# A relational graph convolution on one core: one-hots compared four tiles at a time and weighted on another engine, with buffers, sums and limits in another order

## The chip, the cores and the metric

The kernel runs on one core of one Trainium2 chip. The metric is device time of one execution in microseconds (us). A core has a matrix engine (TensorE, PE in the profile; its weight loads are PEld), VectorE (DVE), ScalarE (ACT), GpSimd (POOL) and a queue that issues DMAs (SP). Each engine takes its own instructions in order; they wait for each other by semaphores. ACT and POOL issue DMAs from their own queues too.

## The reference

Two layers of a relational graph convolution, a residual and a layer norm. There are 12500 nodes with 128 features, 200000 edges sorted by their target, and ten relations; an edge's relation is the argmax of ten of its 42 attributes. For each node and relation the source rows are averaged, and each average is multiplied by that relation's weights:

```python
def _rgcn_layer(x, src, dst, edge_type, w_rel, root, bias):
    N = x.shape[0]
    seg = dst * NUM_REL + edge_type
    xs = x[src]
    sums = jax.ops.segment_sum(xs, seg, num_segments=N * NUM_REL)
    cnt = jax.ops.segment_sum(jnp.ones(seg.shape, x.dtype), seg, num_segments=N * NUM_REL)
    mean = (sums / jnp.maximum(cnt, 1.0)[:, None]).reshape(N, NUM_REL, -1)
    return jnp.einsum('nrd,rdo->no', mean, w_rel) + x @ root + bias
...
edge_type = jnp.argmax(msg[:, NODE_EMB_DIM:-NODE_EMB_DIM], axis=1).astype(jnp.int32)
h = jax.nn.relu(_rgcn_layer(x, src, dst, edge_type, w_rel1, root1, b1))
return _rgcn_layer(h, src, dst, edge_type, w_rel2, root2, b2)
...
x = _layernorm(x + _L0_gnn_ref(...), axis=-1)
```

## The kernel before, in words

The edges are cut into 1563 tiles of 128, one edge per partition. For each tile one indirect DMA, issued by POOL (L827, `gathered`), brings the source rows into a slot of a gather buffer `g`. A one-hot matrix `oh` has, for each edge, its weight (one over the count of its node and relation) in the column of its node and relation: the nodes of a tile span a window of 12, times ten relations gives 120 columns. PE multiplies the gathered rows with it (L1070), into one of four PSUM banks `zp` of two tiles each, and VectorE adds the product to `cc` (L860), the sums by relation, at the tile's offset. That offset is read into a register from `row` (L851), which ACT fetches once in 128 tiles.

Four tiles are a part; there are 391. The loop of `layer_1` over parts writes the order of all engines out by hand. In step p, VectorE makes the one-hots of part p + 1 (`AHEAD`), POOL gathers part p, PE multiplies part p, and VectorE adds the products of part p - 2 (`BEHIND`), half of them ahead of the step's other work and half after. That work comes from `jobs` and `todo`, lists of functions with the tile at which they are due: the preparation of the next 128 tiles' keys, weights and relations, limits for the second layer (`tile_limits`, L486, and `row_limits`), and what follows when the sums of a block of 256 nodes are complete.

A complete block is projected by PE (L820, ten relations), ACT applies the relu (L749), PE multiplies the result with the second layer's weights (L949), ACT brings these products from PSUM to a buffer (L955), and a DMA writes them to the table `TB` in DRAM. The block's place in `cc` is cleared by ACT (L800); at a lap of the ring `cc`, ACT copies its edge (L808).

From tile 177 on (`NX`), a gather takes two rows at once from `TB`: the features, and the second layer's product for that relation, if the source's block is done by then. So the same tile gives a part of the second layer's sum, with a second one-hot of 12 columns by node alone (L838 and L840, product L1074). What is left for the second layer, fewer tiles, follows in `layer_2` (one-hots L834 again, products L1529).

Gather buffers hold eight slots of 128 columns. The first 48 tiles use six buffers, the next up to tile 177 five, and from there four, with four tiles of two slots each. Every second use of a buffer takes its slots from the last to the first (`turn`). The buffers of the one-hots are four (`OB`).

`places` (L366 to L393) computes the tiles' offsets at the start; VectorE's 51 instructions of L373 are its bulk. Its result `b_r` is what `row` is fetched from.

Of the kernel before, what the change touches and what calls it, by code (L numbers as in the profile page):

```python
# [36 lines left out]
AHEAD = 1  # L37
# [33 lines left out]
def rgcn_resnorm_kernel(ctx: ExitStack, tc: tile.TileContext, x, src, dst, attr, w_rel1, root1, b1,  # L71
# [146 lines left out]
    hots_ = [lasting.tile([P, QB * KY], F32, name=f"oh{i}") for i in range(OB)]  # L218
    turn_of_ = {"g": 0, "oh": 0, "ys": 0}
# [115 lines left out]
    nodeP = in_bank(QB * WN)  # L335
# [99 lines left out]
    def shifted_rows(a, b, limit):  # L435

        first = NX // QB * QB if a == NX else a
# [37 lines left out]
    def tile_limits():  # L475
# [7 lines left out]
        for to, first in zip(reach_of, (low_of, high_of)):  # L483
            nc.vector.memset(to, 0.0)
            for i, t in enumerate(first):
                nc.vector.scalar_tensor_tensor(to, u, t - 0.5, to, op0=ALU.is_gt, op1=ALU.add)  # L486
                if i % 8 == 7:
                    yield 1
# [216 lines left out]
    zero = const.tile([P, YB], F32, name="zero")  # L705
# [124 lines left out]
    def hots(keys, weights, cols, n, m, nodes=None):  # L830
# [5 lines left out]
        if nodes is not None:  # L836
            eq = nodeP[:, :n * WN].rearrange("p (t n) -> p t n", n=WN)
            nc.vector.tensor_tensor(eq, nodes[:, :, None].to_broadcast([P, n, WN]),  # L838
                                    cols[:, None, :WN].to_broadcast([P, n, WN]), op=ALU.is_equal)
            nc.vector.tensor_tensor(oh[:, QB * KW:QB * KW + n * WN].rearrange("p (t n) -> p t n", n=WN), eq,  # L840
                                    weights[:, :, None].to_broadcast([P, n, WN]), op=ALU.mult)
# [62 lines left out]
    def layer_1():  # L904
# [107 lines left out]
        jobs.job(80 * QB, tile_limits(), 2 * QB)  # L1012
# [12 lines left out]
        for i, a in enumerate(range(0, RW, YB)):  # L1025
            def wipe(t, a=a):
                m = min(YB, RW - a)
# [3 lines left out]
        used = {}  # L1031
        turn_of_["zp"] = 0
        fixed = [ps_z.tile([P, YB], F32, name=f"zp{i}") for i in range(4)]
        for p in range(-AHEAD, NPT + BEHIND):
            if p + AHEAD < NPT:
                t0, n = parts[p + AHEAD]
                ohs[p + AHEAD] = hots(keyE[:, t0:t0 + n], wE[:, t0:t0 + n], iotaP, n, KW,
                                       nodeE[:, t0 % NODES:t0 % NODES + n] if t0 + n > NX else None)
# [3 lines left out]
            if p < NPT:  # L1042
# [16 lines left out]
                made = (g, ohs.pop(p), slot)  # L1059
            if p == NPT - CP // 4:  # L1060
                xbs[NBLK - 1] = rows_in(NBLK - 1)
                fTs[NBLK - 1] = features_in(NBLK - 1, 0, xbs[NBLK - 1])
            def products(g, oh, slot, a, b):
                n = parts[p][1]
                for j in range(a, min(b, n)):
# [6 lines left out]
                    if i >= NX:  # L1072
                        a = QB * KW + j * WN
# [658 lines left out]
```

## Time and profile before

| | us |
|---|---|
| median of 3 runs | 3123.92 |
| lowest, highest | 3121.44, 3126.94 |
| the profiled execution's own time | 3128.32 |
| its span, first to last instruction | 3126.5 |
| VectorE busy in the span | 2118.9 |
| ACT busy | 370.3 |
| POOL busy | 2296.7 |
| PE busy, and its mean granted clock | 2155.1, 0.683 of full speed |

The profile is of one execution. A row of a group gives the source line, the engine, the operation and its tiles, then the busy time and the mean of one in ns, then the time that the engine was idle just before these instructions, with what ended it (`<-`). "issue" is a wait for nothing that the profile shows. In the timeline a row gives the start, the duration, and in brackets the idle time before. Matmuls are pipelined and their ends are modelled, so a busy PE is not a PE at its peak. An fp32 product is two rows in the counts (x2 for one tile).

### The profile page before, as it was taken

How to read it: one execution, taken by the hardware profiler on the slowest of the kernel's cores; microseconds unless marked ns; L12 is line 12 of the kernel's file. 1: busy time of each engine (PE TensorE's matmuls, PEld its weight loads, DVE VectorE, ACT ScalarE, POOL GpSimd, SP SyncE). 2: the span in 40 equal slices, each digit the busy share in tenths (PEclk: the TensorE clock that was granted, in tenths of full speed). 3: DMA queues.
4: the chain of work that ended last, by engine and by line, in shares of the span. 5: the costliest groups of instructions: out<-in, count | busy, mean ns of one | idle time of the engine just before them, and what ended most of it. 6: DMA issues, size and time to landing. Idle time of an engine off the chain costs nothing.

```text
span 3126.5 us, 37701 instructions
## 1 busy us (share of the span) xinstructions
PE 2155.1 (69%) x10120; PEld 1783.0 (57%) x10120; DVE 2118.9 (68%) x8089; ACT 370.3 (12%) x602; POOL 2296.7 (73%) x2439
## 2 busy tenths in 40 slices
PE   2768787877878787888888888843655555555554
PEld 1546666666767676767676767743554444444443
DVE  6868688888777877777776868479773443434443
ACT  1112111111111111111111111100000000000000
POOL 6777777676777777777777777777777777777775
PEclk8778777776878777777777868855755555555555
DMA  6676667575666666666666655532222222222222
GB/s 183 184 216 185 200 184 232 160 215 158 200 193 196 197 194 197 196 196 196 196 185 192 184 159 146 142 94 60 60 60 63 66 70 66 67 66 70 66 67 56
DMA packets 444103, 454.59 MB, mean 145 GB/s; under 512 B 53110, under 2 KB 376239, under 8 KB 443880
## 3 DMA queue, kind: packets, MB, share of 16 engines
q0 software_dynamic: 99840, 250.04, 28.9%
q1 hardware_dynamic: 303331, 182.87, 19.6%
q10 hardware_dynamic: 40709, 19.15, 2.1%
q8 instruction: 85, 1.39, 0.2%
q14 instruction: 138, 1.13, 0.1%
HBM read 309.45 MB, written 148.80 MB: 147 GB/s over the span
## 4 chain that ended last, share of the span: by engine, by line
DVE 30%; POOL 20%; PE 19%; issue 15%; DMA 11%; DVEq 3%; ACT 1%; SPq 0%; POOLq 0%; ACTq 0%
POOL g L827 20%; DVE oh L834 8%; DVE cc L860 7%; PE pf L820 7%; DMA g<-TB,idxE 5%; PE zp L1070 4%; DVEq L851 3%; DMA g<-TB,idxB 2%; PE yb L949 2%; DMA row<-b_r 2%; PE zp L1074 2%; DVE bank L838 1%; DVE reach L486 1%; DVE acc L1554 1%; DVE cc L1274 1%
## 5 line engine op out<-in xcount | busy, mean ns | idle before, releaser
L827 POOL DMA_INDIRECT g<-TB,idxE x1563 | 1478.6, 946 | 525.8 <-issue 421.2
L1070 PE MATMUL zp<-oh,g 128*128 128x120 f32 x3126 | 822.6, 361 | 367.0 <-DVE cc L860 258.3
L1070 PEld LDWEIGHTS zp<-oh,g 128*128 128x128 f32 x3126 | 601.8, 235 | 523.9 <-DVE cc L860 354.5
L827 POOL DMA_INDIRECT g<-TB,idxB x687 | 649.1, 945 | 209.3 <-issue 199.0
L860 DVE TENSOR_TENSOR cc<-cc,zp 128x132 f32 (+1 forms) x1563 | 453.0, 290 | 373.5 <-PE zp L1074 140.7
L1529 PE MATMUL zy<-oh,g 128*128 128x12 f32 (+23 forms) x1170 | 320.3, 380 | 314.0 <-DMA g<-TB,idxB 211.5
L1074 PEld LDWEIGHTS zp<-oh,g 128*128 128x128 f32 x2772 | 529.7, 238 | 0.0
L834 DVE TENSOR_SCALAR oh<-bank,keyE,wE 128x120 f32<-128x120 f32 x1563 | 517.1, 392 | 0.0
L1529 PEld LDWEIGHTS zy<-oh,g 128*128 128x128 f32 x1170 | 274.3, 310 | 370.4 <-DMA g<-TB,idxB 230.5
L1074 PE MATMUL zp<-oh,g 128*128 128x12 f32 x2772 | 481.6, 249 | 0.0
L820 PE MATMUL pf<-cc,w 128*128 128x256 f32 (+2 forms) x1040 | 306.9, 466 | 6.3 <-DVE cc L860 5.9
L949 PE MATMUL yb<-w,a 128*128 128x512 f32 (+1 forms) x576 | 288.2, 583 | 2.3 <-ACT g L955 1.2
L820 PEld LDWEIGHTS pf<-cc,w 128*128 128x128 f32 x1040 | 250.1, 255 | 55.2 <-issue 5.8
L1529 PE MATMUL zq<-oh,g 128*128 128x16 f32 (+27 forms) x558 | 168.1, 395 | 155.6 <-DMA g<-TB,idxB 141.4
L1529 PEld LDWEIGHTS zq<-oh,g 128*128 128x128 f32 x558 | 138.2, 314 | 188.6 <-DMA g<-TB,idxB 154.2
L827 POOL DMA_INDIRECT g<-in_x_dram,idxE x177 | 167.4, 946 | 74.3 <-issue 50.6
L777 DVE TENSOR_TENSOR cc<-pf,cc 128x256 f32<-128x256 f32 (+2 forms) x52 | 21.2, 409 | 264.4 <-PE pf L1472 264.3
L1554 DVE TENSOR_TENSOR acc<-acc,zy 128x12 f32 (+25 forms) x585 | 104.3, 178 | 105.3 <-PE zy L1529 50.7
L834 DVE TENSOR_SCALAR oh<-columns,keyB,wB 128x15 f32<-128x15 f32 (+25 forms) x687 | 163.8, 322 | 0.1
L783 ACT ACTIVATE rstd<-mv,eps 128x2 f32<-128x2 f32 (+2 forms) x52 | 15.3, 295 | 967.1 <-DVE mv L781 967.0
L749 ACT ACTIVATE a<-pf,b 128x256 f32<-128x256 f32 (+1 forms) x50 | 23.3, 466 | 852.9 <-PE pf L822 852.9
L800 ACT ACTIVATE cc<-zero 128x1280 f32<-128x1280 f32 x90 | 118.8, 1368 | 4.8 <-DVE acc L942 4.8
(265 smaller groups left out, 1807.3 us busy)
## 6 DMA issues: line engine op xcount, KB each, us to landing
TB<-xb SPq DMA_DIRECT2D x88, 640.0 KB
m<-in_edge_attr_dram SPq DMA_DIRECT2D x48, 672.0 KB
TB<-g SPq DMA_DIRECT2D x98, 256.0 KB
g<-TB,idxE POOLq DMA_INDIRECT x1563
TB<-ys SPq DMA_DIRECT2D x96, 256.0 KB
g<-TB,idxB POOLq DMA_INDIRECT x687
TB<-ys SPq DMA_DIRECT2D x49, 128.0 KB
TB<-in_x_dram ACTq DMA_DIRECT2D x12, 512.0 KB
```

The source lines that it names most:

```text
L486: nc.vector.scalar_tensor_tensor(to, u, t - 0.5, to, op0=ALU.is_gt, op1=ALU.add)
L800: nc.scalar.activation(cc[:, r, o:o + n], zero[:, None, :n].to_broadcast([P, m, n]), AF.Copy)
L820: nc.tensor.matmul(po[:, :n], wsb[l][:, r, :], sums[:, r], start=(r == 0), stop=(w is None and r == NREL - 1))
L827: nc.gpsimd.indirect_dma_start(out=g[:, j * C:(j + n) * C], out_offset=None, in_=table, in_offset=bass.IndirectOffsetOnAxis(ap=idx, axis=0))
L834: nc.vector.tensor_scalar(oh[:, j * m:(j + 1) * m], cols[:, :m], keys[:, j:j + 1], weights[:, j:j + 1], op0=ALU.is_equal, op1=ALU.mult)
L851: vals = nc.values_load_multi_w_load_instructions(row, engines=[DVE], min_val=min(a for a, _ in lims), max_val=max(b for _, b in lims), sk ...
L860: nc.vector.tensor_tensor(s, s, zp[:, at:at + m * w].rearrange("c (r n) -> c r n", n=w), op=ALU.add)
L949: nc.tensor.matmul(yb[:h, :m], fin_a[k][:, b * P:b * P + h], wsb[1][:, r:r + m // C, :], start=True, stop=True)
L1070: nc.tensor.matmul(zp[:, o:o + KW], g[:, slot[j] * C:(slot[j] + 1) * C], oh[:, j * KW:(j + 1) * KW], start=True, stop=True)
L1074: nc.tensor.matmul(zp[:, o + KW:o + KY], g[:, (slot[j] + 1) * C:(slot[j] + 2) * C], oh[:, a:a + WN], start=True, stop=True)
L1529: nc.tensor.matmul(zp[:, j * w:(j + 1) * w], g[:, at * C:(at + 1) * C], oh[:, j * w:(j + 1) * w], start=True, stop=True)
L1554: nc.vector.tensor_tensor(s, s, zps[q][:, j * w:(j + 1) * w], op=ALU.add)
```

## The change

Layer 1's one-hots are made in two steps by two engines. `ones` (L842 in the changed kernel) compares the keys of four tiles with the column numbers in one VectorE instruction of 480 columns. `weighted` (L850) then multiplies each tile's 120 columns in place with the edge's weight, on ACT, from the last tile to the first. The comparison runs two parts ahead (`AHEAD` = 2), the weighting one. The one-hots by node get buffers of their own, two, and are made for eight tiles at once (L858 and L860), once in two parts.

All four sums of part p - 2 now stand ahead of the step's other work: two, then the comparison, then two. `finished` keeps what follows them at its old place in PE's order. Gathers of single rows take their slots forwards always. Tile limits are done in groups of four every fourth part, where they were groups of eight every second. The fills with zeros at the start take 256 columns each, where they took 512. Layer 2 has no change of its own.

```diff
-AHEAD = 1
+AHEAD = 2
...
-    hots_ = [lasting.tile([P, QB * KY], F32, name=f"oh{i}") for i in range(OB)]
+    hots_ = [lasting.tile([P, YB], F32, name=f"oh{i}") for i in range(OB)]
+    nhots_ = [lasting.tile([P, 2 * QB * WN], F32, name=f"nh{i}") for i in range(2)]
...
-                if i % 8 == 7:
+                if i % 4 == 3:
                     yield 1
...
-    zero = const.tile([P, YB], F32, name="zero")
+    zero = const.tile([P, BN], F32, name="zero")
...
-    def hots(keys, weights, cols, n, m, nodes=None):
+    def hots(keys, weights, cols, n, m):
...
+    def ones(keys, n):
+
+        oh = next_of("oh", hots_)
+        nc.vector.tensor_tensor(oh[:, :n * KW].rearrange("p (t m) -> p t m", m=KW),
+                                iotaP[:, None, :].to_broadcast([P, n, KW]),
+                                keys[:, :, None].to_broadcast([P, n, KW]), op=ALU.is_equal)
+        return oh
+
+    def weighted(oh, j, w):
+
+        s = oh[:, j * KW:(j + 1) * KW]
+        nc.scalar.activation(s, s, AF.Copy, scale=w)
+
+    def node_hots(t0):
+
+        n = min(2 * QB, NT - t0)
+        a = t0 % NODES
+        oh = next_of("nh", nhots_)
+        eq, to = [b[:, :n * WN].rearrange("p (t n) -> p t n", n=WN) for b in (nodeP, oh)]
+        nc.vector.tensor_tensor(eq, nodeE[:, a:a + n, None].to_broadcast([P, n, WN]),
+                                iotaP[:, None, :WN].to_broadcast([P, n, WN]), op=ALU.is_equal)
+        nc.vector.tensor_tensor(to, eq, wE[:, t0:t0 + n, None].to_broadcast([P, n, WN]), op=ALU.mult)
         return oh
...
-        jobs.job(80 * QB, tile_limits(), 2 * QB)
+        jobs.job(80 * QB, tile_limits(), 4 * QB)
...
         for p in range(-AHEAD, NPT + BEHIND):
+            t = p * QB
+            if 0 <= p < NPT - 1:
+                sums(p, t, 0, 2)
             if p + AHEAD < NPT:
                 t0, n = parts[p + AHEAD]
-                ohs[p + AHEAD] = hots(keyE[:, t0:t0 + n], wE[:, t0:t0 + n], iotaP, n, KW,
-                                       nodeE[:, t0 % NODES:t0 % NODES + n] if t0 + n > NX else None)
+                ohs[p + AHEAD] = ones(keyE[:, t0:t0 + n], n)
+            if 0 <= p + AHEAD - 1 < NPT:
+                t0, n = parts[p + AHEAD - 1]
+                for j in reversed(range(n)):
+                    weighted(ohs[p + AHEAD - 1], j, wE[:, t0 + j:t0 + j + 1])
+            if 0 <= p < NPT - 1:
+                sums(p, t, 2, QB)
+            if p % 2 and p + 1 < NPT and parts[p + 1][0] + QB > NX // (2 * QB) * 2 * QB:
+                nhs[(p + 1) // 2] = node_hots(parts[p + 1][0])
...
-                if not plain or p % 2 == 0:
+                if not plain:
                     turn = used[id(g)] = 1 - used.get(id(g), 1)
-                slot = [p % 2 * QB + j if plain else 2 * j for j in range(n)]
-                if turn:
-                    slot = [GQ - (1 if plain else 2) - a for a in slot]
+                slot = [p % 2 * QB + j if plain else 2 * (n - 1 - j if turn else j) for j in range(n)]
...
             if p < NPT - 1:
-                sums(0, 2)
                 products(*made, 0, 2)
                 todo.run(t - QB // 2)
                 jobs.run(t)
-                sums(2, QB)
+                finished(p, t)
                 products(*made, 2, QB)
```

**VectorE, one step in the middle of layer 1, before.** The step in which a chunk's counts become weights (`wp`); `zp_406` holds the third and fourth tile of part p - 2, `oh_90` is the one-hot buffer of part p + 1, L444 ends the relations of 16 tiles ahead, L636 to L639 are jobs.

```order
L444 ISA idxE<-idxE,moved 128x32
L636 TENSOR_REDUCE cn<-pf 128x128
L638 TENSOR_SCALAR cn<-cn 128x128
L639 RECIPROCAL wp<-cn 128x128
L860 ISA
L860 TENSOR_TENSOR cc<-cc,zp_406 128x11x12
L860 ISA
L860 TENSOR_TENSOR cc<-cc,zp_406 128x11x12
L834 TENSOR_SCALAR oh_90<-bank,keyE,wE 128x120 x4
L838 TENSOR_TENSOR bank<-nodeE,bank 128x48
L840 TENSOR_TENSOR oh_90<-bank,wE 128x48
```

**VectorE, the same step in the changed kernel**, from the load of the offsets (L870) to the first of the same jobs (L431); `zp_430` and `zp_431` are the two banks of part p - 2, and `oh_90` is the buffer of part p + 2.

```order
L870 TENSOR_LOAD row
L879 ISA
L879 TENSOR_TENSOR cc<-cc,zp_430 128x11x12
L879 ISA
L879 TENSOR_TENSOR cc<-cc,zp_430 128x11x12
L842 TENSOR_TENSOR oh_90<-bank,keyE 128x480
L879 ISA
L879 TENSOR_TENSOR cc<-cc,zp_431 128x11x12
L879 ISA
L879 TENSOR_TENSOR cc<-cc,zp_431 128x11x12
L431 TENSOR_SCALAR movedf<-keyE 128x16
```

The second pair of sums stood behind the step's jobs and now stands ahead of them; one comparison of 480 columns stands between the pairs in place of four instructions of 120 after them, and the pair of 48 columns is gone from this step.

**ACT around a finished block of 256 nodes, before** (`fT` the block's features, `a` the relu behind its projection, `ys` and `g` the buffers of the second layer's products).

```order
L800 ACTIVATE cc<-zero 128x6x256
L990 ACTIVATE fT<-pf 128x256
L749 ACTIVATE a<-pf,b_385 128x256
L955 ACTIVATE ys_106<-yb 128x512
L955 ACTIVATE ys_107<-yb 128x512
L955 ACTIVATE g_89<-yb 128x256
```

**ACT around such a block in the changed kernel** (`oh_90` to `oh_93` the one-hot buffers of four parts in turn).

```order
L801 ACTIVATE cc<-zero 128x6x256
L850 ACTIVATE oh_93<-oh_93,wE 128x120 x4
L1009 ACTIVATE fT<-pf 128x256
L850 ACTIVATE oh_90<-oh_90,wE 128x120 x4
L850 ACTIVATE oh_91<-oh_91,wE 128x120 x4
L850 ACTIVATE oh_92<-oh_92,wE 128x120 x4
L750 ACTIVATE a<-pf,b_410 128x256
L850 ACTIVATE oh_93<-oh_93,wE 128x120 x4
L974 ACTIVATE ys_108<-yb 128x512
L974 ACTIVATE ys_109<-yb 128x512
L850 ACTIVATE oh_90<-oh_90,wE 128x120 x4
```

Four weightings for each part now stand between the instructions that follow PE, in the same queue.

**VectorE at the start, before**: the first chunk's weights, then `places` (L366 and on), into which the first one-hots are laid one by one; the pattern of the last rows goes on for 16 one-hots.

```order
L636 TENSOR_REDUCE cn<-pf 127x128
L638 TENSOR_SCALAR cn<-cn 127x128
L639 RECIPROCAL wp<-cn 127x128
L286 COPY wE<-pf 128x127
L366 TENSOR_TENSOR off<-b_i,even 13x128
L369 MEMSET lows 13x128
L834 TENSOR_SCALAR oh_90<-bank,keyE,wE 128x120
L373 SCALAR_TENSOR_TENSOR lows<-even,lows 13x128
```

**VectorE at the start in the changed kernel.**

```order
L618 TENSOR_TENSOR eqb<-bank,kh 127x1344 x5
L842 TENSOR_TENSOR oh_90<-bank,keyE 128x480
L842 TENSOR_TENSOR oh_91<-bank,keyE 128x480
L637 TENSOR_REDUCE cn<-pf 127x128
L842 TENSOR_TENSOR oh_92<-bank,keyE 128x480
L639 TENSOR_SCALAR cn<-cn 127x128
L842 TENSOR_TENSOR oh_93<-bank,keyE 128x480
L640 RECIPROCAL wp<-cn 127x128
L287 COPY wE<-pf 128x127
L367 TENSOR_TENSOR off<-b_i,even 13x128
L370 MEMSET lows 13x128
L374 SCALAR_TENSOR_TENSOR lows<-even,lows 13x128 x46
```

The comparisons need no weights, so they moved ahead of them, and nothing stands between the instructions of `places` any more.

More of the change, by code (lines that the diff above doesn't have):

```diff
@@ L1072, in products @@
                     if i >= NX:
[L1073 to L1074 removed]
+                        a = (i % (2 * QB)) * WN
+                        nc.tensor.matmul(zp[:, o + KW:o + KY], g[:, (slot[j] + 1) * C:(slot[j] + 2) * C], nh[:, a:a + WN],
                                          start=True, stop=True)
[L1077 to L1102 removed]
             if p < NPT - 1:
[L1105 removed]
                 products(*made, 0, 2)
@@ L1112, in layer_1 @@
                 jobs.run(t)
-                sums(0, QB)
+                sums(p, t, 0, QB)
+                finished(p, t)
                 if p < NPT:
```

79 lines of the change are left out of this document (38 added, 41 removed).

## The prediction, made before the changed kernel had run

> **What bounds the kernel now.** I read the page's span and groups first, then a table by stage, then POOL's own timeline and waits, and last the stretch around POOL's longest wait. The gathers are the groups to begin with; the columns are line, engine, operation, tiles and count, then busy time and mean ns, then the idle time ahead of them.
>
> ```profile
> span 3126.5 us, 37701 instructions
> PE 2155.1 (69%) x10120; PEld 1783.0 (57%) x10120; DVE 2118.9 (68%) x8089; ACT 370.3 (12%) x602; POOL 2296.7 (73%) x2439
> L827 POOL DMA_INDIRECT g<-TB,idxE x1563 | 1478.6, 946 | 525.8 <-issue 421.2
> L827 POOL DMA_INDIRECT g<-TB,idxB x687 | 649.1, 945 | 209.3 <-issue 199.0
> L827 POOL DMA_INDIRECT g<-in_x_dram,idxE x177 | 167.4, 946 | 74.3 <-issue 50.6
> ```
>
> A gather holds POOL 0.945 us. Where nothing stops it (the second layer, x687) 209.3/687 = 0.305 us lie ahead of each, called issue: one gather per 1.250 us. All 1563 + 687 + 177 = 2427 then need 3034 us of a span of 3126.5. POOL, busy 73% by the page, is within 3% of being the only bound, and a gain is at most what POOL loses beyond that pace. The table says where it does (stretch and length, then busy us and counts, PE's granted clock, DMA share, GB/s):
>
> ```profile
> 390.00:790.00 400.00, 315.40 (x1597) 262.26 (x1596) 334.99 (x1324) 63.56 (x94) 275.41 (x292) 0.75 0.65 190
> 790.00:1700.00 910.00, 748.52 (x3880) 631.92 (x3880) 694.84 (x2505) 159.07 (x233) 686.84 (x727) 0.77 0.66 195
> 1700.00:1910.00 210.00, 175.69 (x873) 145.85 (x874) 161.84 (x566) 34.62 (x52) 152.20 (x161) 0.76 0.57 164
> 2060.00:3100.00 1040.00, 537.43 (x1916) 440.56 (x1917) 543.30 (x2361) 17.52 (x54) 786.51 (x833) 0.52 0.25 64
> ```
>
> POOL's count is the fifth bracket. Lost time is length minus count times 1.250: 400 - 365 = 35 us in the first row, 910 - 909 = 1 in the second, 210 - 201 = 9 in the third, nothing in the fourth (833 gathers fit to the edge). So the second layer has nothing to give or lose, and layer 1 lost 45 us in two stretches. The rest is at two points:
>
> ```profile
> 83.14 0.94 POOL L827 DMA_INDIRECT g<-in_x_dram,idxE  x1 [19.06 <-PE zp L1070]
> 2040.77 0.94 POOL L827 DMA_INDIRECT g<-TB,idxE  x1 [3.19 <-DMA rowP<-b_i]
> 3105.82 0.94 POOL L827 DMA_INDIRECT g<-TB,idxB  x1 [0.30 <-issue]
> ```
>
> The start costs 19.06 - 0.30 = 18.8 us, the change of layers 2.9. After the last gather come 3126.5 - 3105.8 = 20.7 us of tail. Lost in all: 18.8 + 35 + 1 + 9 + 3 = 67 us. Who holds POOL in the first stretch:
>
> ```profile
> POOL g L827 <- PE zp L1074: 36.2, 16, 7.6
> 540.45 0.78 PE L1070 MATMUL zp<-oh,g 128*128 128x120 f32 x2 [5.15 <-DVE cc L860]
> 551.87 6.54 PE L820 MATMUL pf<-cc,w 128*128 128x256 f32 x20
> 559.91 0.94 POOL L827 DMA_INDIRECT g<-TB,idxE  x1 [7.55 <-PE zp L1074]
> ```
>
> 16 waits of 36.2 us are for a product to free a gather buffer (four buffers of four tiles: a lead of 16 tiles, 20 us). PE was late because VectorE's sums (L860) were late with the PSUM banks, 5.15 us at one wait, and a block's projection (6.54 us) then came on top. VectorE is busy 335 of 400 us there and 695 of 910 (76%) in the next stretch, where POOL loses 1 us. Its load is what tells the two apart: the clock (0.75, 0.77) does not.
>
> **The one-hots.** Per part (four tiles) VectorE loses four compares and, once relations are split by node, two small products. The rows:
>
> ```profile
> 1006.75 1.32 DVE L834 TENSOR_SCALAR oh<-bank,keyE,wE 128x120 f32<-128x120 f32 x4
> L838 DVE TENSOR_TENSOR bank<-nodeE,bank 128x48 f32<-128x48 f32 x347 | 73.7, 212 | 11.8
> L840 DVE TENSOR_TENSOR oh<-bank,wE 128x48 f32<-128x48 f32 x347 | 71.9, 207 | 11.9
> L617 DVE TENSOR_TENSOR eqb<-bank,kh 128x1344 bf16<-128x1344 f32 (+2 forms) x65 | 100.7, 1551 | 1.3 <-PE pf L628 0.7
> L486 DVE SCALAR_TENSOR_TENSOR reach<-u,reach 128x6 f32<-128x6 f32 x252 | 42.2, 167 | 7.6
> ```
>
> The new compare is the form of L838 and L617 (both operands broadcast or stepped, one from PSUM) with 480 columns; no row has that width. Between 48 and 1344 columns a column costs (1551 - 212)/1296 = 1.03 ns, so 212 + 432 x 1.03 = 0.66 us; bounds are 0.21 and 1.55. I take 0.66, by the line through both. It saves 1.32 - 0.66 = 0.66 us a part; at 1.55 it would lose 0.23. Node one-hots for eight tiles at once cost 2 x (0.21 + 48 x 0.00103) = 0.52 us instead of 4 x 0.21, which saves 0.16 a part. Together 0.82 us of the 5.0 us that four gathers take. The tile limits (L486, 42.2 us) were done in steps of 8 every second part and now come in steps of 4 every fourth: of those 42 us about 30 leave the stretch for later parts.
>
> So VectorE has in 390 to 790: 335 - 73 parts x 0.82 - 30 = 245 of 400 us, 61%, below the 76% at which POOL loses 1 us in 910. In 1700 to 1910: 162 - 40 x 0.82 = 129 of 210, 61% as well (77% before). Sums of a part's third and fourth tile also move ahead of the step's other jobs, so PE's second half no longer waits behind those. I leave 4 of the 35 us and 2.5 of the 9 standing, for blocks where PE itself is late: 31 + 6.5 saved.
>
> **ACT's new work**, 1563 activations of 128x120 with a scale per partition. Nearest rows:
>
> ```profile
> L749 ACT ACTIVATE a<-pf,b 128x256 f32<-128x256 f32 (+1 forms) x50 | 23.3, 466 | 852.9 <-PE pf L822 852.9
> L990 ACT ACTIVATE fT<-pf 128x256 f32<-128x256 f32 (+1 forms) x50 | 18.6, 373 | 150.5 <-PE pf L983 150.5
> 2036.88 0.30 ACT L1202 ACTIVATE cc<-zero 127x128 f32<-127x128 f32 x1
> 2037.08 0.30 ACT L1203 ACTIVATE cc<-zero 127x128 f32<-127x128 f32 x1
> 393.32 0.60 ACT L955 ACTIVATE g<-yb 128x512 f32<-128x512 f32 x1 [5.25 <-PE yb L949]
> ```
>
> Two zero fills follow each other here: 2037.08 - 2036.88 = 0.20 us is the pitch of such short operations, the lower bound; 0.47 us (L749, twice as wide, a column operand as here) is the upper. L749 over L990 puts the column operand at 0.09 us, so I take 0.30: 1.2 us a part (0.8 to 1.9), of 5.0. ACT's 370 us on the page become some 840, 40% of layer 1. It is covered because the compare runs two parts ahead and the weighting one: a product finds weights that ACT began a part earlier. Queued behind a waiting ACT instruction (the relu behind a projection, an eviction that waits up to 5.25 us for PE) are the weights of a part whose products stand one to three parts further on in PE's order; without that cover 1.2 us would fall on PE in every part.
>
> **The start.** The 49th gather goes to the second buffer. Before, the slots were taken backwards there, so it waits for the product of tile 15; now forwards, for tile 8.
>
> ```profile
> 53.38 0.38 DVE L834 TENSOR_SCALAR oh<-bank,keyE,wE 128x120 f32<-128x120 f32 x1
> 53.89 0.38 DVE L834 TENSOR_SCALAR oh<-bank,keyE,wE 128x120 f32<-128x120 f32 x1
> 54.21 9.67 DVE L373 SCALAR_TENSOR_TENSOR lows<-even,lows 13x128 f32<-13x128 f32 x31
> 73.67 0.59 DVE L860 TENSOR_TENSOR cc<-cc,zp 128x120 f32 x2 [5.11 <-issue]
> 74.31 1.21 PE L1070 MATMUL zp<-oh,g 128*128 128x120 f32 x4 [23.30 <-DVE cc L860]
> 81.65 1.21 PE L1070 MATMUL zp<-oh,g 128*128 128x120 f32 x4 [1.52 <-DVE cc L860]
> ```
>
> Tiles 8 and 9 are the products at 74.31, tiles 14 and 15 those at 81.65. The first sum waits for the places of the tiles (L373 and on). 16 one-hots stood between these, each adding 0.51 - 9.67/31 = 0.20 us: 3.2 us. The four compares now stand ahead: two in a wait for PE, two (1.3 us) before the weights are done. So the first sum comes at 73.67 - 1.9 = 71.8, and tile 8's product ends 0.64 + 0.61 later, at 73.0: gather 49 starts some 9.5 us earlier (bounds: 0, if ACT's weights come late, and 18.8). Later tiles follow at less than the 1.25 us a gather needs, so it stays. Short wipes of zeros (256 columns instead of 512) lie on ACT before 46 us, when nothing waits for ACT: no cost, or up to 1.2 us, one part's weights.
>
> **Sum:** 9.5 + 31 + 6.5 = 47 us off the span. The profiled execution took 3128.3 us (span 3126.5), the median of the runs is 3123.9; taken off that: 3077 us.
>
> **Rivals.** *PE keeps the bound (3104).* Two speeds stand in the rows:
>
> ```profile
> 716.39 0.78 PE L1070 MATMUL zp<-oh,g 128*128 128x120 f32 x2 [3.89 <-DVE cc L860]
> 733.50 0.46 PE L1070 MATMUL zp<-oh,g 128*128 128x120 f32 x2
> L1074 PE MATMUL zp<-oh,g 128*128 128x12 f32 x2772 | 481.6, 249 | 0.0
> L820 PE MATMUL pf<-cc,w 128*128 128x256 f32 (+2 forms) x1040 | 306.9, 466 | 6.3 <-DVE cc L860 5.9
> L949 PE MATMUL yb<-w,a 128*128 128x512 f32 (+1 forms) x576 | 288.2, 583 | 2.3 <-ACT g L955 1.2
> ```
>
> Slow, four tiles take 4 x 0.78 = 3.1 us; L1074, L820 and L949 add (482 + 307 + 288)/391 parts = 2.8 us a part, so a PE that stayed slow would need 5.9 of the 5.0 us that there are. If PE, waiting less for VectorE, waits for gathers instead and stays slow, only a quarter of the 37.5 us goes: 3124 - 9.5 - 10 = 3104. Against it: from 790 to 1700 the clock is the same and POOL loses 1 us. [...]
>
> *ACT's queue becomes the bound (slower, 3169).* If the weights come more than a part (5.0 us) behind the compare, because they sit behind evictions that wait for PE, PE waits at the next part and POOL loses its lead. One part's weights and an eviction, 1.2 + 0.6 us, at each of 50 blocks (x50 at L749) are 92 us: 3077 + 92 = 3169. For it: ACT already waits up to 5.25 us at an eviction, and its instructions run in one order. Against it: ACT is busy 64 of 400 us now, and the queue order leaves two parts.
>
> *It does not do what it says (3124).* The compare at 1.1 us or more leaves VectorE's load where it was, and the start's wait only moves.
>
> **How the numbers follow.** Forecast 0.66, by itself 3064 (both stretches wholly won, 44 us, and 16 at the start) to 3092 (two thirds of the 47); PE's bound 0.17; no effect 0.05; ACT's queue 0.12. Range 3060 to 3116: it holds nearly all of the first two (0.63 + 0.17), and so leaves out 0.20. What this kernel's runs can tell from no change is about 0.2%, 6 us. Faster 0.83, same 0.05, slower 0.12.
>
> **What would show it.** Right: a compare of about 0.66 us (L842) and four weightings within 1.2 us; gather 49 near 73.5 us; 390 to 790 with some 316 gathers; POOL's waits for the products (L1132, which is L1074 before) below 10 us there; the last 1040 us unchanged. Wrong: POOL or PE waiting for L850, a VectorE busy over 75% in 390 to 790, or the same waits for products with the clock at 0.75 or less.

## The result, and the profile after

| | before | after |
|---|---|---|
| median, us | 3123.75 (4 runs) | 3076.23 (4 runs) |
| lowest, highest | 3121.44, 3126.94 | 3074.45, 3076.94 |
| span of the profiled execution | 3126.5 | 3075.1 |

The ratio is 0.9846, with a 95% interval of 0.9829 to 0.9863: 47.5 us faster, where 47 were forecast. The page of the changed kernel begins as follows (busy time, share of the span, instructions), and its groups for gathers, compare, weights and products have the columns of the rows shown before:

```profile
span 3075.1 us, 38388 instructions
PE 2162.1 (70%) x10120; PEld 1810.3 (59%) x10120; DVE 1782.8 (58%) x6571; ACT 824.8 (27%) x2190; POOL 2296.1 (75%) x2439
...
L828 POOL DMA_INDIRECT g<-TB,idxE x1563 | 1478.5, 946 | 487.5 <-issue 407.6
L1128 PE MATMUL zp<-oh,g 128*128 128x120 f32 x3126 | 825.2, 362 | 317.0 <-DMA g<-TB,idxE 183.9
...
L850 ACT ACTIVATE oh<-oh,wE 128x120 f32<-128x120 f32 x1563 | 482.1, 383 | 217.4 <-DVE oh L842 198.5
...
L842 DVE TENSOR_TENSOR oh<-bank,keyE 128x480 f32<-128x480 f32 x391 | 255.3, 653 | 399.4 <-PE zp L1128 365.4
```

VectorE has lost 336 us of work and ACT has gained 454. A compare of 480 columns takes 653 ns (0.66 us was the estimate). The gather is what it was, 946 ns, and POOL's busy time too (2296.1 us, 2296.7 before): all that was won was POOL's waiting. The table by stretches, with the columns of the one before (POOL's count is the fifth bracket):

```profile
390.00:790.00 400.00, 330.57 (x1699) 283.02 (x1698) 247.54 (x877) 158.66 (x413) 298.79 (x316) 0.76 0.69 202
790.00:1700.00 910.00, 765.88 (x3920) 655.42 (x3920) 576.81 (x1992) 367.50 (x958) 686.76 (x727) 0.75 0.66 194
1700.00:1910.00 210.00, 184.59 (x920) 154.41 (x920) 118.59 (x389) 85.90 (x228) 158.86 (x168) 0.76 0.58 165
2010.00:3050.00 1040.00, 534.66 (x1904) 437.96 (x1904) 540.85 (x2360) 17.53 (x54) 786.28 (x833) 0.52 0.25 64
```

Between 390 and 790 there are now 316 gathers, so 400 - 316 x 1.25 = 5 us are lost there; 727 fit in the second row as before, 168 x 1.25 fill the third, and layer 2 has the same 833. POOL's longest waits that are left, and the last gather, stand in the timeline (start, duration, the idle time ahead in brackets):

```profile
70.50 0.94 POOL L828 DMA_INDIRECT g<-in_x_dram,idxE  x1 [6.49 <-PE zp L1128]
...
535.08 0.94 POOL L828 DMA_INDIRECT g<-TB,idxE  x1 [5.03 <-PE zp L1132]
...
1989.10 0.94 POOL L828 DMA_INDIRECT g<-TB,idxE  x1 [4.19 <-DMA rowP<-b_i]
...
3054.42 0.94 POOL L828 DMA_INDIRECT g<-TB,idxB  x1 [0.30 <-issue]
```

| POOL's loss, us | before | forecast after | after |
|---|---|---|---|
| start (49th gather) | 18.8 | 9.3 | 6.2 |
| 390 to 790 | 35 | 4 | 5 |
| 790 to 1700 | 1 | 1 | 1 |
| 1700 to 1910 | 9 | 2.5 | 0 |
| change of layers | 2.9 | 2.9 | 3.9 |
| after the last gather | 20.7 | 20.7 | 20.7 |

The rows add up to a gain of 51 us; the spans differ by 51.4. (A window that is the same in us holds somewhat later tiles in the changed kernel, which is over 40 us ahead by 1700.) PE's waits before layer 1's products show why the stretches closed (what is waited for, us in all, times, the longest). First the kernel before, then the changed one:

```profile
PE zp L1070 <- DVE cc L860: 258.3, 205, 23.3
...
PE zp L1070 <- DMA g<-TB,idxE: 93.0, 92, 2.8
```

```profile
PE zp L1128 <- DMA g<-TB,idxE: 183.9, 191, 3.6
...
PE zp L1128 <- DVE cc L879: 30.0, 29, 2.4
PE zp L1128 <- ACT oh L850: 12.4, 11, 1.6
```

PE waited 258 us for VectorE's sums; now it waits 30 us for them, 12 us for ACT's weights, and mostly, 184 us, for the gathers, which at 1.25 us each take 3034 of the span's 3075.1 us. A part of the fall is a change of name: PE's first long wait at the start, 23.3 us and put down to the sums before, is still there with 18.3 us, but is called issue. In all, PE's idle time ahead of these products fell from 367.0 to 317.0 us.

### The profile page after: what moved, and what is told of

Its sections match the earlier page's. It is cut to its first block, busy times and chain, and to the rows that moved or that the text cites. A ratio compares the mean times of both kernels' runs of the same rounds, so it can differ in the third digit from the quotient of the medians.

```text
span 3075.1 us, 38388 instructions
## 1 busy us (share of the span) xinstructions
PE 2162.1 (70%) x10120; PEld 1810.3 (59%) x10120; DVE 1782.8 (58%) x6571; ACT 824.8 (27%) x2190; POOL 2296.1 (75%) x2439
## 4 chain that ended last, share of the span: by engine, by line
PE 31%; POOL 22%; DMA 16%; issue 15%; DVE 13%; ACT 2%; DVEq 1%; POOLq 0%; ACTq 0%; SPq 0%
POOL g L828 22%; DMA g<-TB,idxE 11%; PE zp L1128 10%; PE pf L821 9%; PE yb L968 4%; PE zp L1132 4%; DMA g<-TB,idxB 3%; DVE cc L879 2%; DMA row<-b_r 1%; DVE oh L835 1%; DVEq L870 1%; DVE acc L1585 1%; DVE cc L1305 1%; PE pf L1340 1%; PE pf L627 1%
## 5 line engine op out<-in xcount | busy, mean ns | idle before, releaser
L1128 PE MATMUL zp<-oh,g 128*128 128x120 f32 x3126 | 825.2, 362 | 317.0 <-DMA g<-TB,idxE 183.9
L1128 PEld LDWEIGHTS zp<-oh,g 128*128 128x128 f32 x3126 | 614.1, 239 | 453.1 <-issue 149.9
L1132 PEld LDWEIGHTS zp<-nh,g 128*128 128x128 f32 x2772 | 543.8, 244 | 0.0
L850 ACT ACTIVATE oh<-oh,wE 128x120 f32<-128x120 f32 x1563 | 482.1, 383 | 217.4 <-DVE oh L842 198.5
L1132 PE MATMUL zp<-nh,g 128*128 128x12 f32 x2772 | 491.0, 252 | 0.0
L842 DVE TENSOR_TENSOR oh<-bank,keyE 128x480 f32<-128x480 f32 x391 | 255.3, 653 | 399.4 <-PE zp L1128 365.4
L750 ACT ACTIVATE a<-pf,b 128x256 f32<-128x256 f32 (+1 forms) x50 | 23.3, 465 | 439.2 <-PE pf L823 439.2
```

Source lines behind the costliest of these rows:

```text
L842: nc.vector.tensor_tensor(oh[:, :n * KW].rearrange("p (t m) -> p t m", m=KW), iotaP[:, None, :].to_broadcast([P, n, KW]), keys[:, :, None] ...
L850: nc.scalar.activation(s, s, AF.Copy, scale=w)
L1128: nc.tensor.matmul(zp[:, o:o + KW], g[:, slot[j] * C:(slot[j] + 1) * C], oh[:, j * KW:(j + 1) * KW], start=True, stop=True)
L1132: nc.tensor.matmul(zp[:, o + KW:o + KY], g[:, (slot[j] + 1) * C:(slot[j] + 2) * C], nh[:, a:a + WN], start=True, stop=True)
```

## The experiments

Twelve runs followed, of ten kernels, on four chips; the table keeps the runs of one chip together. On none of these did the kernel before take the time of the first measurement: its medians there are 3777, 3817, 3827 and 3778 us. The last two sections come back to that. So whole times are compared within one chip only, and the mechanism is read from places that are the same on all chips (the start) or from waits.

The waits have a limit of their own. The profile names what ended a wait from the records of semaphores, and the twelve traces hold 16584 to 18679 of these, where the first two hold 59558 and 60986. That a wait whose record is missing may be called issue or remote, or go by another name, is my guess and was not tested; to be safe, a sum of waits by name in the twelve is not to be set against one of the first two traces. Between traces of the same steady code such sums scatter too: on one chip PE waits 62.4 us for the weights in changed_again and 86.9 in places_early, and on two chips 182.9 and 136.2 us for ACT's evictions (the moves of the second layer's products out of PSUM) in the changed kernel itself.

| kernel | median, us | before, same chip | ratio, 95% interval |
|---|---|---|---|
| undo_turn | 3762.4 | 3777.3 | 0.9963 (0.9947 to 0.9979) |
| undo_limits | 3755.9 | 3777.3 | 0.9938 (0.9917 to 0.9960) |
| undo_sums | 3754.9 | 3777.3 | 0.9929 (0.9904 to 0.9955) |
| hots_alone | 3768.7 | 3777.3 | 0.9987 (0.9970 to 1.0003) |
| changed_again | 3808.0 | 3817.3 | 0.9986 (0.9970 to 1.0002) |
| three_compares | 3856.5 | 3817.3 | 1.0102 (1.0077 to 1.0126) |
| act_twice | 3855.8 | 3817.3 | 1.0110 (1.0090 to 1.0130) |
| places_early | 3810.6 | 3817.3 | 0.9986 (0.9970 to 1.0002) |
| hots_alone_2 | 3834.3 | 3827.4 | 1.0026 (1.0006 to 1.0046) |
| orders_alone | 3819.4 | 3827.4 | 0.9983 (0.9963 to 1.0002) |
| weights_early | 3756.9 | 3778.4 | 0.9932 (0.9906 to 0.9957) |
| changed_third | 3749.9 | 3778.4 | 0.9920 (0.9896 to 0.9943) |

**One part of the change undone.** undo_turn takes the slots as before, undo_limits the old pace of the limits, undo_sums the old place of a part's second two sums; hots_alone undoes all three, and keeps the new one-hots. Each by its core:

```diff
-                slot = [p % 2 * QB + j if plain else 2 * (n - 1 - j if turn else j) for j in range(n)]
+                slot = [p % 2 * QB + j if plain else 2 * j for j in range(n)]
+                if turn:
+                    slot = [GQ - (1 if plain else 2) - a for a in slot]
```

```diff
-                if i % 4 == 3:
+                if i % 8 == 7:
...
-        jobs.job(80 * QB, tile_limits(), 4 * QB)
+        jobs.job(80 * QB, tile_limits(), 2 * QB)
```

```diff
-            if 0 <= p < NPT - 1:
-                sums(p, t, 2, QB)
...
                 jobs.run(t)
+                sums(p, t, 2, QB)
                 finished(p, t)
```

> The changed kernel with the slots of the single-row gathers taken backwards at every second use again. Theory (the 49th gather waits for the product of tile 15 instead of tile 8): the wait before gather 49 grows from 6.5 us to 11 to 14 us, nothing else changes, about 6 us slower (ratio to before 0.986 to 0.988). Rival (the start was won by the comparisons that left the chain of the places, the slots give nothing): the wait stays at 6.5 us, ratio 0.984 to 0.985.

> The changed kernel with the tile limits in groups of eight every second part again, so that all 42 us of them fall between 400 and 770 us. Theory (VectorE's share of the stretch decides, and the one-hots alone lower it enough): VectorE about 275 of 400 us in 390 to 790 (69%), POOL loses 5 to 10 us there instead of 5, ratio 0.984 to 0.987. Rival (the spreading of the limits is what freed the stretch): POOL loses 15 us or more there, ratio 0.988 or above.

> The changed kernel with the second pair of sums behind the step's jobs again. Theory (the load decides, not the order): POOL loses at most 5 us more in 390 to 790, ratio 0.984 to 0.986. Rival (PE's second half was late because its bank came behind the jobs): POOL loses 15 us or more more, ratio 0.989 or above.

> The changed kernel with all three undone (slots, limits, order of the sums): of the change only the one-hots in two steps, the node one-hots for eight tiles and the shorter fills are left. Theory (the one-hots' relief of VectorE carries the stretches): POOL's loss in 390 to 790 is 5 to 12 us, the start loses 11 to 16 us, ratio 0.987 to 0.990. Rival (the orders carry it): POOL loses 25 us or more in 390 to 790, ratio 0.994 or above.

The whole times expected were for a chip at 3124 us, and cannot be held against these. All four are faster than before or level with it. Among the first three, undo_limits and undo_sums are level; hots_alone is slower than both (its interval lies above theirs). What each undone part costs cannot be told, since the changed kernel itself did not run on that chip. What the traces show is the start and PE's waits; both are read below, with the counterpart.

**The one-hots alone again, and the orders alone.** orders_alone is the kernel before with the changed slots, limits and place of the sums, and its own one-hots:

```diff
-                if i % 8 == 7:
+                if i % 4 == 3:
...
-        jobs.job(80 * QB, tile_limits(), 2 * QB)
+        jobs.job(80 * QB, tile_limits(), 4 * QB)
...
-                slot = [p % 2 * QB + j if plain else 2 * j for j in range(n)]
-                if turn:
-                    slot = [GQ - (1 if plain else 2) - a for a in slot]
+                slot = [p % 2 * QB + j if plain else 2 * (n - 1 - j if turn else j) for j in range(n)]
...
                 sums(0, 2)
+                sums(2, QB)
                 products(*made, 0, 2)
```

> The new one-hots and ACT's weights with the old slots, the old pace of the limits and the old order of the sums, for the second time. Where the kernel before takes about 3124 us: VectorE has 247.5 + 30 = 278 of 400 us between 390 and 790 (69%, still below the 76% at which POOL lost 1 us in 910), so by the theory (VectorE's load sets that stretch) POOL loses at most 10 us there, and at the start some 6 us more than in the changed kernel, as gather 49 waits for tile 15 again: 3080 to 3090 us. Rival (the order and the slots made the gain): over 3105 us. Where the kernel before takes over 3700 us: within 10 us of it, as the first time (ratio 0.999).

> The counterpart: the kernel before with its own one-hots on VectorE, but with the changed slots, the limits spread over twice the parts, and the sums of a part's third and fourth tile ahead of the step's other jobs. Where the kernel before takes about 3124 us: the start gains 6 us by the slots; VectorE has 335 - 30 = 305 of 400 us between 390 and 790 (76%), at the edge of what POOL bore from 790 on, so by the theory 10 to 25 of the 35 us lost there go: 3093 to 3108 us, above the kernel with the one-hots alone. Rival (the one-hots made nearly all of it): 3112 to 3120 us. Where the kernel before takes over 3700 us, the undone limits and sums alone seemed worth -10 to -15 us there, so 0 to 15 us above the kernel before.

On this chip the orders alone come out 8 us below the kernel before, where 0 to 15 above were expected, and the one-hots alone 7 us above it. The orders alone are thus the faster by 15 us, with intervals that do not meet: that the one-hots are the part with the gain is not what times on this chip show.

The start, from the timelines: the issue of the row that the first sum needs, the first sum, the 49th gather. The changed kernel of the first measurement (its 49th gather, at 70.50, is shown above); then changed_again, undo_turn, undo_sums, hots_alone_2 and orders_alone:

```profile
65.39 0.58 ACTq L1058 DMA_DIRECT2D row<-b_r  x1
...
68.78 0.59 DVE L879 TENSOR_TENSOR cc<-cc,zp 128x120 f32 x2 [3.42 <-issue]
```

```profile
87.37 0.58 ACTq L1058 DMA_DIRECT2D row<-b_r  x1
...
92.47 0.95 POOL L828 DMA_INDIRECT g<-in_x_dram,idxE  x1 [28.59 <-PE zp L1128]
```

```profile
88.10 0.58 ACTq L1058 DMA_DIRECT2D row<-b_r  x1
...
98.62 0.94 POOL L828 DMA_INDIRECT g<-in_x_dram,idxE  x1 [34.76 <-PE zp L1130]
```

```profile
87.67 0.58 ACTq L1058 DMA_DIRECT2D row<-b_r  x1
...
92.77 0.95 POOL L828 DMA_INDIRECT g<-in_x_dram,idxE  x1 [28.93 <-PE zp L1126]
```

```profile
87.55 0.58 ACTq L1058 DMA_DIRECT2D row<-b_r  x1
90.94 0.59 DVE L879 TENSOR_TENSOR cc<-cc,zp 128x120 f32 x2 [3.42 <-issue]
...
100.62 0.95 POOL L828 DMA_INDIRECT g<-in_x_dram,idxE  x1 [36.63 <-PE zp L1128]
```

```profile
90.63 0.60 ACTq L1083 DMA_DIRECT2D row<-b_r  x1
...
95.55 1.29 DVE L860 TENSOR_TENSOR cc<-cc,zp 128x120 f32 x4 [4.96 <-issue]
...
97.25 0.94 POOL L827 DMA_INDIRECT g<-in_x_dram,idxE  x1 [33.43 <-PE zp L1068]
```

From the row to the 49th gather it is 5.11 us in the changed kernel of the first measurement and 5.10 in changed_again: the traces differ before the row, not after it. So the start can be taken apart. Before it was 83.14 - 68.59 = 14.55 (row issue in that trace at 68.59). The one-hots alone leave 13.07 (1.5 won: the first sum follows the row by 3.4 us instead of 5). The sums' place then brings 13.07 to 10.52 (2.5), the slots 10.52 to 5.10 (5.4, where 4.5 to 7.5 were expected). These two are not independent: undo_sums, which has the changed slots and the old place of the sums, has 5.10 as well. With the slots forwards the 49th gather does not need the second pair of sums, and the slots alone win all 8 us there; two gathers later the old place costs 0.9. The row itself comes 90.63 - 87.55 = 3.1 us earlier with the new one-hots, on one chip. Together 12.5 us, and 83.14 - 70.50 = 12.6 were won in the first measurement. orders_alone gives the slots and the sums' place together from the other side: 97.25 - 90.63 = 6.62 is 14.55 less 7.9, and 2.5 + 5.4 = 7.9.

PE's waits for the sums, of orders_alone, hots_alone_2, undo_sums, undo_turn and three_compares (the changed kernel with each compare made three times; it comes next) in this order:

```profile
PE zp L1068 <- DVE cc L860: 229.5, 70, 23.1
```

```profile
PE zp L1128 <- DVE cc L879: 71.2, 38, 7.7
```

```profile
PE zp L1126 <- DVE cc L879: 85.1, 53, 4.2
```

```profile
PE zp L1130 <- DVE cc L879: 12.1, 7, 4.0
```

```profile
PE zp L1134 <- DVE cc L885: 28.0, 24, 3.7
```

Without the new one-hots the changed orders leave 230 us of waits for sums. With them 71 are left (87.5 in the first run of hots_alone), and with the sums' new place as well about 10 (12.1 in undo_turn; undo_limits has 9.2 and the changed kernel itself 3.4 and 11.1 in its two runs). So the new one-hots and the sums' place both take these waits away, and the slots and the pace of the limits do not touch them.

That it is VectorE's load which makes them, as the theory has it, these traces speak against. three_compares keeps VectorE busy for 2289.6 us, orders_alone for 2122.4, and yet the first has 28.0 us of such waits and the second 229.5 (on two chips, whose times for the kernel before differ by 10 us). What else tells the two apart is the order: with the old one-hots VectorE makes a part's one-hots (1.32 us, and twice 0.21 for those by node) right ahead of its four sums; with the new ones two sums come first, and the compare is made two parts ahead. No run takes order and load apart any further, and none has VectorE as full as it was in the first measurement: 335 of the 400 us from 390 on there, 282 of the same 400 in three_compares. Nor do these waits set the time on these chips: undo_sums, with 85 us of them, and undo_limits, with 9, take 3754.9 and 3755.9 us on the same chip. PE's idle time moves there rather than goes. Ahead of layer 1's products and ahead of the second layer's it is, on one chip, in orders_alone and then in hots_alone_2:

```profile
L1068 PE MATMUL zp<-oh,g 128*128 128x120 f32 x3126 | 851.7, 371 | 375.9 <-DVE cc L860 229.5
L949 PE MATMUL yb<-w,a 128*128 128x512 f32 (+1 forms) x576 | 372.6, 736 | 204.5 <-ACT g L955 90.0
```

```profile
L1128 PE MATMUL zp<-oh,g 128*128 128x120 f32 x3126 | 859.9, 375 | 275.4 <-issue 112.3
L968 PE MATMUL yb<-w,a 128*128 128x512 f32 (+1 forms) x576 | 367.9, 728 | 340.5 <-ACT g L974 141.4
```

The one-hots alone have 100 us less than the orders alone at the first, and 136 us more at the second.

**VectorE's load, ACT's load, and the places earlier.** three_compares makes each compare three times, act_twice follows each weighting by a second activation, places_early calls `places` ahead of the counts of the first 128 tiles:

```diff
                                 keys[:, :, None].to_broadcast([P, n, KW]), op=ALU.is_equal)
+        nc.vector.tensor_tensor(oh[:, :n * KW].rearrange("p (t m) -> p t m", m=KW),
+                                iotaP[:, None, :].to_broadcast([P, n, KW]),
+                                keys[:, :, None].to_broadcast([P, n, KW]), op=ALU.is_equal)
+        nc.vector.tensor_tensor(oh[:, :n * KW].rearrange("p (t m) -> p t m", m=KW),
+                                iotaP[:, None, :].to_broadcast([P, n, KW]),
+                                keys[:, :, None].to_broadcast([P, n, KW]), op=ALU.is_equal)
```

```diff
         nc.scalar.activation(s, s, AF.Copy, scale=w)
+        nc.scalar.activation(s, s, AF.Copy, scale=1.0)
```

```diff
     checked(0, d_f)
+    places()
     pc = None
...
-    places()
     weights_in()
```

> The changed kernel itself, beside the others of this call, so that they are read against it on one and the same chip. Where the kernel before takes about 3124 us, 3076 us again (ratio 0.985). Where it takes about 3777 us, as in the first four experiments, POOL waits of some 4 us per 24 gathers run through both layers; if these leave the change its own part of the gain, 3777 - 48 = 3729 us; if they cover part of it (the four undone versions gained 9 to 22 us there), 3740 to 3756 us.

> Slots, limits, order of sums and ACT's weights as in the changed kernel, but each part's compare is made three times: 2 x 0.653 = 1.31 us more of VectorE per part, 79 parts in the 400 us from 390 on, so VectorE's 247.5 us there become some 350 of 400 (88%; the kernel before had 335), and in the 910 us after it 577 + 182 x 1.31 = 815 (90%; before 695). Theory (VectorE's load set the loss between 390 and 790): POOL loses at least the 35 us of before there and now loses in the next stretch too, so at least 3076 + 30 + 10 = 3116 us, up to 3160. Rival (the slots, the limits' pace and the order of the sums made the gain, VectorE's load is covered): within 6 us of the changed kernel.

> Each weighting on ACT is followed by a second activation of the same tile: ACT's 0.29 to 0.38 us per tile become twice that, 2.5 us a part instead of 1.25, ACT's busy time 825 us becomes some 1300 (about 65% of layer 1). Theory (ACT has slack, the weights are made a part ahead): within 6 us of the changed kernel, with the start up to 2.5 us later. Rival (ACT's queue is close to the bound): PE waits for the weights at each block, 50 blocks x 1 to 2 us: 50 to 100 us slower.

> The places of the tiles (46 small VectorE operations, 14.4 us) are worked out before the counts of the first chunk rather than after them, so that they, and the row that the first sum loads, no longer come last before the first sum. Theory (the 6.2 us that POOL still waits ahead of the 49th gather are a chain of VectorE work, row, first sum, product): the weights come up to 14 us later, the sums' places are no longer the last; if the weights of the first parts then come before the row did, gather 49 starts up to 6 us earlier, 3070 us (6 under the changed kernel). Rival (the weights now end last: the same VectorE work stands ahead of the first product either way): no change within 6 us, with PE's first product later and its wait at gather 49 as long as before.

The second rows of the pages of changed_again, three_compares and act_twice:

```profile
PE 2184.9 (57%) x10120; PEld 1840.8 (48%) x10120; DVE 1787.3 (47%) x6571; ACT 823.3 (22%) x2190; POOL 2302.3 (60%) x2439
```

```profile
PE 2199.5 (57%) x10120; PEld 1844.8 (48%) x10120; DVE 2289.6 (59%) x7353; ACT 827.8 (21%) x2190; POOL 2296.3 (59%) x2439
```

```profile
PE 2153.5 (56%) x10120; PEld 1815.2 (47%) x10120; DVE 1786.1 (46%) x6571; ACT 1286.4 (33%) x3753; POOL 2295.8 (60%) x2439
```

502 us more of VectorE cost 48 us at the end, which lies in the theory's range of 40 to 84 over the changed kernel; the rival, VectorE's load being covered, falls. But the cost did not come the way the theory has it. PE's waits for the sums are 28.0 us instead of 3.4; its waits for ACT's evictions are 234 instead of 183, while ACT waits 254 us for the compares instead of 90. That the late compares held ACT's queue, and the evictions in it, would explain this, and was not tested. 463 us more of ACT cost 48 us too: there the theory was wrong and the rival nearly right. PE's waits for the weights in changed_again, then in act_twice:

```profile
PE zp L1128 <- ACT oh L850: 62.4, 21, 6.2
```

```profile
PE zp L1129 <- ACT oh L851: 133.3, 41, 6.9
```

In act_twice another 26.9 us are waits for the first of the two activations (L850). On these chips ACT's queue does hold PE (62.4 us in changed_again), at an engine that is busy 22% of the span there. An estimate from these runs follows. A us of VectorE's work is worth 48/502 = 0.096 us there, and one of ACT's 48/463 = 0.104. The change takes 336 us from VectorE and gives ACT 454, so these two come to -32 + 47 = +15 us, against 12.6 won at the start: little in all. Measured are -9 us on one chip and -28 on another, and hots_alone at -9 and +7. The estimate explains that the gain is smaller than 47.5 us, and no more.

places_early moved nothing: its row is issued at 87.45 us (87.37 in changed_again), and gather 49 starts at 92.55 (92.47). 27 of the 46 operations still ran behind the counts in VectorE's order, so it tells neither for nor against a start bound by the places.

**The weights a part earlier.**

```diff
-            if 0 <= p + AHEAD - 1 < NPT:
-                t0, n = parts[p + AHEAD - 1]
+            if p + AHEAD < NPT:
                 for j in reversed(range(n)):
-                    weighted(ohs[p + AHEAD - 1], j, wE[:, t0 + j:t0 + j + 1])
+                    weighted(ohs[p + AHEAD], j, wE[:, t0 + j:t0 + j + 1])
```

> ACT weights a part in the step in which VectorE compares it, two parts ahead of its products instead of one. On the chips of the experiments PE waits 62 us for the weights (21 times, up to 6.2 us), and 133 us where each weighting is followed by a second activation, which made the kernel 48 us slower: there 0.67 us of the end per us of PE's wait. Theory (part of what the new one-hots save is given back because the weights stand behind evictions in ACT's queue): with 5 us more lead PE's wait for weights falls below 25 us, and the kernel is 15 to 30 us faster than the changed kernel of the same call. Rival (ACT's stalls, not its order, take the time; and ACT, now waiting for the compare of the same step, delays the evictions behind it): no gain, PE's waits for the evictions (183 us) grow by what those for the weights lose, within 8 us of the changed kernel. Where the kernel before takes about 3124 us PE waits only 12.4 us for the weights: within 5 us of 3076 us.

> The changed kernel, for the comparison with the weights a part earlier. 3076 us where the kernel before takes 3124; where it takes over 3750 us, 0.994 to 1.000 of that.

PE's waits for ACT in changed_third, then in weights_early:

```profile
PE yb L968 <- ACT g L974: 81.8, 21, 6.6
PE yb L968 <- ACT ys L974: 54.4, 18, 7.2
PE zp L1128 <- ACT oh L850: 49.1, 21, 6.2
```

```profile
PE yb L968 <- ACT ys L974: 94.4, 25, 7.6
PE yb L968 <- ACT g L974: 86.4, 23, 7.0
...
PE zp L1127 <- ACT oh L850: 13.5, 7, 5.5
PE zp L1127 <- DVE cc L879: 56.2, 21, 8.7
```

The waits for the weights fall by 36 us, as the theory said, and the gain it forecast does not come: the median is 7 us above the changed kernel's, with intervals that overlap. The rival's forecast holds. Its reason is less sure. The waits for the evictions are 45 us longer than in changed_third, but at 181 us no longer than in changed_again (183); and the waits for the sums grew as much, from 11.1 to 56.2 us. So what the weights won was lost at other waits, and one trace of each does not tell at which. No kernel that ran beside the changed one on its chip beats it.

## Why the prediction was right

**The bound.** Right. POOL's busy time (2296.7 and 2296.1 us) and the pace of a gather (833 in 1040 us of layer 2 both times) did not move, and the gain is the sum of its waits (51 us of 51.4 in the span).

**The one-hots, 31 us.** Right in size: 35 to 5 us in that stretch, VectorE at 247.5 us there (245 forecast). PE's waits for sums went as the prediction has it in the first two traces (258.3 to 30.0 us). Its reason, VectorE's load, is not shown: three_compares has more load than orders_alone (2289.6 us against 2122.4) and an eighth of its waits for sums (28.0 against 229.5), which points to what stands ahead of the sums in VectorE's order. The 30 us of limits that I moved out of the stretch are not seen to matter: undoing their pace left PE's waits at 9 us. The place of the sums did (85 to about 10), and the prediction named it without a size of its own. That PE's waits for the sums made the 30 us of POOL's loss was not tested by an experiment on a chip at 3124 us; it rests on the two first traces.

**The late stretch, 6.5 us.** It won all 9: VectorE fell to 118.6 of 210 us, not 129. What made this loss no run shows by itself.

**The start, 9.5 us.** The mechanism was right, the term too small: 12.6. The row came 3.2 us earlier (68.59 to 65.39), where 1.9 was taken, since the four compares did not lengthen VectorE's way to the row (the weights were copied at 45.65, and at 45.79 before); and the first sum followed the row by 3.4 us instead of 5.1, which was not foreseen. In both traces of kernels with the old one-hots ACT's queue issued two transfers of 512 KB right behind the row (row at 68.59 us, transfers at 69.27 and 69.87 before; 90.63, 91.30 and 91.90 in orders_alone); with the new ones four weightings (1.25 us) and a fill (0.40) stand between. That these slowed the row's transfer is a guess; no run tests it.

**ACT.** Four weightings in 1.25 us (1.2 forecast), 824.8 us on the page (840). Its queue held PE for 12.4 us in all, so the rival of 3169 us did not come. (By its own terms it was 3167: 50 blocks at 1.8 us are 90 us, not 92.) On the four other chips PE's waits for the weights were 46 us and more wherever the weights stood as in the changed kernel, so it came there in part.

**The sum.** 47 us were to come off the span, 51.4 did. That the median still came out within a us is luck: the profiled execution of before took 4.4 us more than its median, and that of the changed kernel 0.7 more. Within the sum the start was 3 us too small and the late stretch 2.5, while the long stretch and the change of layers came out a us worse each. What was confirmed is the way of counting POOL's losses by place.

**The rivals.** PE's slow speed: from 390 to 790 the clock was 0.76 (0.75 before) and POOL was not held (5 us lost); over all of layer 1 PE waited twice as long for gathers as before (183.9 us against 93.0), and its products took 362 ns (361 before). What remains of POOL's waits for products between 390 and 790 is 11.4 us in 21 waits, a little over the 10 that were named as a sign, and 6 of it is the usual 0.30 us ahead of a gather. The longest, 5.0 us at 535.08, follows a block's projection (6.92 us from 526.66), which came after ACT had copied the ring's edge (1.78 us from 520.85). That the change does nothing: excluded by the interval.

## What to carry to other kernels

Where one engine's fixed pace is within a few per cent of the whole time, list its waits by stretch and ask for each which engine is late there. The load of that engine in a stretch that loses nothing gave a forecast of the right size here, but not a cause: ask also what stands ahead of the late instruction in its engine's order. Work that is moved to an idle engine is not free because its share is low: it goes into a queue with others (ACT was busy 12% of the span before; the weights that it was given then held PE for 12.4 us, and for 62.4 in changed_again). And a gain holds for the conditions under which the bound was read: 47.5 us became 9 and 28 in two later measurements, so measure before and after more than once, on more than one chip.

## What the runs showed of the hardware that was not expected

The same program took 3076 us in the first measurement, 3808 on one chip and 3750 on another. Most instructions are as long (the compare 653 and 654 ns, the gather 946 and 949 in the first measurement and in changed_again); PE's products of layer 1 took 362 and 370 ns, at a mean granted clock of 0.679 and 0.654. Layer 2's gathers, in code that no edit touched, have 344.8 us of idle time ahead of them in changed_again, where the first measurement had 209:

```profile
L828 POOL DMA_INDIRECT g<-TB,idxB x687 | 650.3, 947 | 344.8 <-issue 196.6 <-remote 80.6 <-PE zy L1560 38.7
```

VectorE there waits for what the profile cannot name ("remote"), in groups that waited for nothing of the kind in the first trace:

```profile
DVE oh L842 <- remote: 264.2, 79, 10.6
DVE acc L1585 <- remote: 250.3, 63, 14.4
DVE cc L879 <- remote: 242.3, 64, 9.8
```

```profile
63.64 0.69 DVE L637 TENSOR_REDUCE cn<-pf 127x128 f32<-127x512 f32 x1 [18.31 <-remote]
```

This one wait makes most of the 22 us by which the row is later there. What is late is open: the DMA queues moved the same packets and bytes in both, and the transfers of an instruction queue took about as long each (84 of 16 KB, 1.16 us on average against 1.11). The name remote itself may say little, as these are the traces with less than a third of the semaphore records: of the landings of DMAs, 10709 are recorded in changed_again and 50200 in the first trace. Why they are fewer is not known either. No run tells whether it is the chip or something else that differed between the measurements.
